# A fused pair of row layers on one core: the third stage issued in program order, ten rows deep, with the right matrix applied to four row sums at once

## The chip, the cores and the metric

The kernel runs on one core of one Trainium2 chip. The metric is the device time in microseconds of one execution. Times of single instructions come from one profiled execution. "PE" is TensorE (matmuls), "PEld" its weight loads, "DVE" VectorE, "ACT" ScalarE, "POOL" GpSimd, "SP" the engine from which the DMA transfers are issued.

## The reference

The input x has the shape 1×384×384×128, in float32: rows i, columns j, 128 channels. Two layers are applied, one after the other.

```python
# layer 0
z = layernorm(x) ; left = (z@Wl+bl)*sigmoid(z@Wlg+blg) ; right = (z@Wr+br)*sigmoid(z@Wrg+brg)
core = einsum('bikh,bjkh->bijh', left, right)
x1 = x + sigmoid(x@Wg+bg) * (layernorm(core)@Wout + bout)
# layer 1, on x1
left = x1@W_left + b_left + x1@W_eq + b_eq
right_sum = sum over j of (x1@W_right + b_right)        # one vector for each row i
out = (left * right_sum * sigmoid(x1@W_gate + b_gate)) @ W_out + b_out
y = layernorm(out + x1) * ln_scale + ln_bias
```

Since the sum over j and the product with W_right can change places, a row needs only its 128 channel sums ("tot") multiplied by W_right ("rsum").

## The kernel before, in words

There are three stages. The first normalises x and writes left and right to DRAM. The second multiplies them channel by channel, writes core to DRAM and gathers what the normalisation of core needs. The third, which the change touches, runs over the 384 rows i. It holds a row transposed, with the channels on the 128 partitions and the 384 columns j along the free dimension, and does the rest of layer 0 and all of layer 1.

A row passes through these steps. The names are those of the tiles, the line numbers those of the profile.

- L361, L363: three PE transposes of x into the PSUM tile pxt, and ACT's copy of it to xT. L364: POOL multiplies core by its reciprocal deviation, cs.
- L303, L305: PE multiplies xT by Wg into pg; ACT takes the sigmoid, gT.
- L324, L325, L328: PE multiplies cs by the output matrix into pr; DVE multiplies by gT, then adds xT, which gives x1T and, as a by-product, its sum over j, tot.
- L309, L315, L317: PE multiplies the one column tot by the right matrix; DVE adds the bias, rsum; ACT scales the output matrix with it, wo.
- L310, L313, L311, L319: PE multiplies x1T by the gate matrix into pg2 (the profile shows it as pg, too) and by the left matrix into pl; ACT takes the sigmoid g2; DVE forms u.
- L341, L342: for each of three blocks of 128 columns, PE multiplies u by wo into py and adds the transposed x1T to it. Py has the columns j on the partitions. L347, L349: DVE's statistics of py.
- L351, L352, L355: for every two rows, POOL forms the reciprocal deviations rs, and DVE nm, which is minus the mean times rs.
- L370, L373, L376: ACT normalises py in three instructions, DVE multiplies by the scale, POOL adds the bias, into yt.

Rows are loaded and stored four at a time from SP. The function tick(t) writes down, for one value of t, the steps of six rows: r0 is row t, r1 row t-1, and so on up to r5. Each step belongs to one of these. The rows overlap in this way, and a step's input was mostly made a tick before. The order in the text is pg of r1, layer 1's products of r2, pr of r1, py of r3, the transposes of r0, and the normalisation of r5.

The order of issue on each engine is not that of the text. The kernel is built with `schedule_with_timeline_sim=True`: a scheduler orders each engine's instructions by a simulated time, within the dependencies. Each tile name of a pool rotates over the pool's number of buffers; all products of the third stage but py share one rotation of four PSUM banks ("bank"), and py has four banks of its own.

Of the kernel before, what the change touches and what calls it, by code (L numbers as in the profile page):

```python
# [8 lines left out]
F32 = mybir.dt.float32  # L9
AF = mybir.ActivationFunctionType  # L10
ALU = mybir.AluOpType
# [3 lines left out]
P = 128  # L15
EPS = 1e-5
# [3 lines left out]
def triangle_then_gated_row_kernel(ctx: ExitStack, tc: tile.TileContext, a: dict, out: bass.AP):  # L20
# [18 lines left out]
    RG = 4  # L39
# [3 lines left out]
    lr_d = dpool.tile([H, N, N, 2], F32, name="lr_d")  # L43
    core_d = dpool.tile([N, H, N], F32, name="core_d")
    rstd_d = dpool.tile([N, N], F32, name="rstd_d")


    def const(shape, name):
# [2 lines left out]
    def load(dst, src):  # L51
        nc.sync.dma_start(out=dst, in_=src)
# [11 lines left out]
    ident = const([P, P], "ident")  # L64
# [25 lines left out]
    wc = const([P, C], "wc")  # L90
    bz = const([P, 1], "bz")
    with tc.tile_pool(name="prep", bufs=1) as pp, tc.tile_pool(name="prep_ps", bufs=1, space=PSUM) as ps:
# [3 lines left out]
        d = pp.tile([P, 1], F32, name="d")  # L96
# [29 lines left out]
    with tc.tile_pool(name="p1x", bufs=3) as xp, tc.tile_pool(name="p1lr", bufs=2) as lrp, \  # L126
# [5 lines left out]
        loaded, normed = {}, {}  # L132
# [135 lines left out]


    with tc.tile_pool(name="p3in", bufs=3) as inp, tc.tile_pool(name="p3out", bufs=3) as op, \  # L270
         tc.tile_pool(name="p3w", bufs=4) as wp, tc.tile_pool(name="p3s", bufs=4) as sp, \
# [6 lines left out]
        def work(name):  # L278
            return wp.tile([P, N], F32, tag=name, name=name)
# [4 lines left out]
        loaded, rows, yts, pair = {}, {}, {}, {}  # L284

        def load_rows(i0):
            if i0 < N:
                xt = inp.tile([P, RG, NB, C], F32, tag="xt", name="xt")
                load(xt, x[i0:i0 + RG].rearrange("i (b p) c -> p i b c", p=P))
                ct = inp.tile([P, RG, N], F32, tag="ct", name="ct")  # L290
                load(ct, core_d[i0:i0 + RG].rearrange("i h j -> h i j"))
                rt = inp.tile([P, RG, N], F32, tag="rt", name="rt")
                load(rt.rearrange("p i j -> p (i j)"),
                     rstd_d[i0:i0 + RG].rearrange("i j -> (i j)").partition_broadcast(P))
                loaded[i0] = xt, ct, rt

        def tick(t):

            r0, r1, r2, r3, r4, r5 = (rows.get(t - d) for d in range(6))
            if r1:  # L300

                pg = bank("pg")
                nc.tensor.matmul(pg[:, :N], lhsT=wg0, rhs=r1["xT"], start=True, stop=True)  # L303
                gT = work("gT")
                nc.scalar.activation(gT, pg[:, :N], AF.Sigmoid, bias=bg0)  # L305
            if r2:

                pl, pg2 = bank("pl"), bank("pg2")
                nc.tensor.matmul(pl[:, N:N + 1], lhsT=wright, rhs=r2["tot"], start=True, stop=True)  # L309
                nc.tensor.matmul(pg2[:, :N], lhsT=wgate, rhs=r2["x1T"], start=True, stop=True)  # L310
                nc.tensor.matmul(pl[:, :N], lhsT=wleft, rhs=r2["x1T"], start=True, stop=True)  # L311
                g2 = work("g2")
                nc.scalar.activation(g2, pg2[:, :N], AF.Sigmoid, bias=bgate)  # L313
                rsum = sp.tile([P, 1], F32, tag="rsum", name="rsum")
                nc.vector.tensor_add(rsum, pl[:, N:N + 1], bright)  # L315
                wo = wp.tile([P, C], F32, tag="wo", name="wo")
                nc.scalar.activation(wo, wout1, AF.Copy, scale=rsum)  # L317
                u = work("u")
                nc.vector.scalar_tensor_tensor(u, pl[:, :N], bleft, g2, ALU.add, ALU.mult)  # L319
                r2.update(u=u, wo=wo)  # L320
            if r1:

                pr = bank("pr")
                nc.tensor.matmul(pr[:, :N], lhsT=wc, rhs=r1["cs"], start=True, stop=True)  # L324
                nc.vector.scalar_tensor_tensor(pr[:, :N], pr[:, :N], bz, gT, ALU.add, ALU.mult)  # L325
                x1T = work("x1T")
                tot = sp.tile([P, 1], F32, tag="tot", name="tot")
                nc.vector.scalar_tensor_tensor(  # L328
                    x1T, pr[:, :N], bout1, r1["xT"], ALU.add, ALU.add, accum_out=tot
                )  # L330
                r1.update(x1T=x1T, tot=tot)
            if r3:

                m, n = divmod(t - 3, 2)
# [4 lines left out]
                py = ps2.tile([P, 512], F32, tag="py", name="py")  # L339
                for s in cols:  # L340
                    nc.tensor.matmul(py[:, s], lhsT=r3["u"][:, s], rhs=r3["wo"], start=True, stop=False)  # L341
                    nc.tensor.matmul(  # L342
                        py[:, s], lhsT=r3["x1T"][:, s], rhs=ident, start=False, stop=True, is_transpose=True
                    )
                st = sp.tile([P, NB, 6], F32, tag="st", name="st")
                for b in range(NB):
                    nc.vector.bn_stats(st[:, b, :], py[:, cols[b]])  # L347
                for b in range(NB):
                    nc.vector.bn_aggr(mv[:, n, b, :], st[:, b, :])  # L349
                if n == 1:  # L350
                    nc.gpsimd.tensor_scalar(rs, mv[:, :, :, 1], EPS, 1.0, ALU.add, ALU.mult)  # L351
                    nc.gpsimd.tensor_tensor(  # L352
                        rs, rs, mhalf[:, :2 * NB].rearrange("p (a b) -> p a b", b=NB), ALU.pow
                    )
                    nc.vector.scalar_tensor_tensor(nm, mv[:, :, :, 0], -1.0, rs, ALU.mult, ALU.mult)  # L355
                r3.update(py=py, rs=rs[:, n], nm=nm[:, n])
            if r0:

                pxt = bank("pxt")
                for b, s in enumerate(cols):  # L360
                    nc.tensor.transpose(pxt[:, s], r0["x"][:, b, :], ident)  # L361
                xT, cs = work("xT"), work("cs")
                nc.scalar.copy(xT, pxt[:, :N])  # L363
                nc.gpsimd.tensor_tensor(cs, r0["c"], r0["r"], ALU.mult)  # L364
                r0.update(xT=xT, cs=cs)
            if r5:

                py, yt = r5["py"], r5["y"]
                for b, s in enumerate(cols):
                    nc.scalar.activation(  # L370
                        py[:, s], py[:, s], AF.Identity, bias=r5["nm"][:, b:b + 1], scale=r5["rs"][:, b:b + 1]
                    )
                nc.vector.tensor_tensor(  # L373
                    yt, py[:, :N].rearrange("p (b c) -> p b c", b=NB), lnsb, ALU.mult
                )
                nc.gpsimd.tensor_tensor(yt, yt, lnbb, ALU.add)  # L376

        load_rows(0)
        load_rows(RG)
        for t in range(N + 5):  # L380
            if t < N:
                r = t % RG
                if r == 0:
                    load_rows(t + 2 * RG)
                    xt, ct, rt = loaded.pop(t)
                    yt = op.tile([P, RG, NB, C], F32, tag="yt", name="yt")
                    yts[t] = yt
                rows[t] = {"x": xt[:, r], "c": ct[:, r], "r": rt[:, r], "y": yt[:, r]}
            tick(t)
            done = t - 5  # L390
            rows.pop(done, None)
            if done >= 0 and done % RG == RG - 1:
                i0 = done - RG + 1
                nc.sync.dma_start(out=y[i0:i0 + RG].rearrange("i (b p) c -> p i b c", p=P), in_=yts.pop(i0))


_INS = [
# [26 lines left out]
```

## Time and profile before

| what | value |
|---|---|
| time, median of 3 runs | 3922.84 us (3920.99 to 3922.89) |
| the profiled execution's own time | 3925.36 us |
| its span, first to last instruction | 3923.6 us |
| mean granted TensorE clock | 0.974 |
| second stage, first to last matmul | 1398 to 2180 us |
| third stage, from its first transpose on | 2208 us to the end |
| busy from 2300 to 2500 us | PE 198.98, DVE 152.56, ACT 138.95, POOL 123.99 us of 200 |
| core busy over the span | PE 93%, DVE 71%, ACT 50%, POOL 32% |

In the profile's slices a digit is the busy share in tenths of one fortieth of the span, some 98 us. A group of instructions is listed as line, engine, operation, output and inputs, shapes and count, then its busy time in us and the mean duration of one in ns, then the idle time of the engine just ahead of it, with what ended that. A line of the timeline has the start in us, the duration, the engine, the line and the number of instructions merged into it; in brackets the idle time before it. Matmuls are pipelined: one starts before the last one's recorded end, so that the distance between starts, not the duration, is what one takes of PE.

### The profile page before, as it was taken

How to read it: one execution, taken by the hardware profiler on the slowest of the kernel's cores; microseconds unless marked ns; L12 is line 12 of the kernel's file. 1: busy time of each engine (PE TensorE's matmuls, PEld its weight loads, DVE VectorE, ACT ScalarE, POOL GpSimd, SP SyncE). 2: the span in 40 equal slices, each digit the busy share in tenths (PEclk: the TensorE clock that was granted, in tenths of full speed). 3: DMA queues.
4: the chain of work that ended last, by engine and by line, in shares of the span. 5: the costliest groups of instructions: out<-in, count | busy, mean ns of one | idle time of the engine just before them, and what ended most of it. 6: DMA issues, size and time to landing. Idle time of an engine off the chain costs nothing.

```text
span 3923.6 us, 46929 instructions
## 1 busy us (share of the span) xinstructions
PE 3668.2 (93%) x14222; PEld 2190.0 (56%) x14222; DVE 2768.9 (71%) x9123; ACT 1952.0 (50%) x3815; POOL 1272.4 (32%) x1304
## 2 busy tenths in 40 slices
PE   7888998998898879999999699999999999999998
PEld 3444443444443345555555466666676676667665
DVE  7878888887887724444444577777777777777776
ACT  2333333333333323333333366666666666666666
POOL 2111111111111100000000266666666666666665
PEclk9999999999999989999999899999999999999999
DMA  3575565565466499999999555555565655556562
GB/s 92 164 200 143 156 199 160 148 199 169 140 194 172 137 287 292 291 293 290 292 290 290 195 170 185 175 180 183 172 192 166 190 173 182 178 177 186 170 192 82
DMA packets 802259, 759.46 MB, mean 194 GB/s; under 512 B 13524, under 2 KB 703704, under 8 KB 802008
## 3 DMA queue, kind: packets, MB, share of 16 engines
q1 hardware_dynamic: 802008, 756.47, 63.6%
q8 instruction: 114, 1.87, 0.2%
q14 instruction: 137, 1.12, 0.1%
HBM read 453.84 MB, written 302.58 MB: 193 GB/s over the span
## 4 chain that ended last, share of the span: by engine, by line
PE 63%; DVE 19%; DMA 16%; ACT 1%; POOL 1%; SPq 0%; issue 0%; POOLq 0%; DVEq 0%; ACTq 0%
PE pc L239 20%; DMA xt<-in_x_dram 15%; PE py L341 8%; PE pg L303 7%; PE pg L310 7%; DVE lr L186 7%; PE pr L324 6%; PE pl L311 6%; DVE st L151 5%; DVE z L165 4%; PE pxt L361 3%; PE py L342 3%; DVE mv L153 2%; PE pr L182 1%; PE pl L309 1%; DMA lr_d<-lr 1%
## 5 line engine op out<-in xcount | busy, mean ns | idle before, releaser
L182 PE MATMUL pr<-wz,zt 128*128 128x512 f32 x2304 | 1098.9, 615 | 137.0 <-DVE lr L186 134.9
L239 PE MATMUL pc<-lrh 128*128 128x384 f32 x2304 | 782.2, 500 | 37.9 <-DMA lrh<-lr_d 37.9
L184 ACT ACTIVATE sg<-pr 128x512 f32<-128x512 f32 x576 | 343.9, 597 | 842.6 <-PE pr L182 755.5
L182 PEld LDWEIGHTS pr<-wz,zt 128*128 128x128 f32 x2304 | 417.4, 195 | 607.5 <-issue 383.2
L364 POOL TENSOR_TENSOR cs<-ct,rt 128x384 f32<-128x384 f32 x384 | 384.3, 1001 | 912.2 <-ACT gT L305 874.3
L239 PEld LDWEIGHTS pc<-lrh 128*128 128x128 f32 x2304 | 448.1, 195 | 372.2 <-issue 41.1
L186 DVE TENSOR_TENSOR lr<-pr,sg 128x512 f32<-128x512 f32 x576 | 588.6, 1027 | 36.4 <-ACT sg L184 36.4
L248 DVE TENSOR_TENSOR csum<-csum,ct 128x1152 f32<-128x1152 f32 x128 | 173.9, 1358 | 486.0 <-ACT ct L245 486.0
L376 POOL TENSOR_TENSOR yt<-yt,lnb 128x384 f32<-128x384 f32 x384 | 374.9, 997 | 393.8 <-DVE yt L373 390.9
L370 ACT ACTIVATE py<-py,nm,rs 128x128 f32<-128x128 f32 x1152 | 435.4, 442 | 53.3 <-DVE nm L355 53.3
L341 PE MATMUL py<-wo,u 128*128 128x128 f32 x2304 | 431.7, 287 | 1.1 <-DVE u L319 0.9
L245 ACT COPY ct<-pc 128x1152 f32<-128x1152 f32 x128 | 143.3, 1119 | 525.2 <-PE pc L239 525.2
L341 PEld LDWEIGHTS py<-wo,u 128*128 128x128 f32 x2304 | 346.2, 190 | 41.4 <-ACT wo L317 2.3
L155 POOL TENSOR_SCALAR rs<-mv 128x16 f32<-128x16 f32 x72 | 14.7, 204 | 1079.3 <-DVE mv L153 1079.3
L165 DVE TENSOR_SCALAR z<-xt,mv,rs 128x128 f32<-128x128 f32 x1152 | 324.2, 338 | 42.9 <-PE pt L168 42.9
L305 ACT ACTIVATE gT<-pg,col_L_conv_bg 128x384 f32<-128x384 f32 x384 | 229.1, 597 | 251.1 <-PE pg L303 251.1
L151 DVE BATCH_NORM_STATS2 st<-xt 128x6 f32<-128x128 f32 x1152 | 253.2, 275 | 138.7 <-DMA xt<-in_x_dram 138.5
L303 PE MATMUL pg<-xT,mat_L_conv_Wg 128*128 128x384 f32 x768 | 332.4, 515 | 12.3 <-ACT xT L363 12.3
L310 PE MATMUL pg<-x1T,mat_L_conv_W_gate 128*128 128x384 f32 x768 | 343.2, 529 | 0.0
L342 PE MATMUL py<-ident,x1T 128*128 128x128 f32 x1152 | 314.0, 273 | 0.0
L324 PE MATMUL pr<-cs,wc 128*128 128x384 f32 x768 | 312.0, 488 | 2.1 <-POOL cs L364 2.1
L311 PE MATMUL pl<-x1T,mat_L_conv_W_left 128*128 128x384 f32 x768 | 311.2, 487 | 0.0
(78 smaller groups left out, 4763.8 us busy)
## 6 DMA issues: line engine op xcount, KB each, us to landing
lr_d<-lr SPq DMA_DIRECT2D x18, 8192.0 KB, 31.1
lrh<-lr_d SPq DMA_DIRECT2D x128, 1152.0 KB, 9.1
core_d<-ct SPq DMA_DIRECT2D x128, 576.0 KB, 3.8
xt<-in_x_dram SPq DMA_DIRECT2D x96, 768.0 KB, 8.2
ct<-core_d SPq DMA_DIRECT2D x96, 768.0 KB, 8.8
rt<-rstd_d SPq DMA_DIRECT2D x96, 768.0 KB, 7.2
out_dram<-yt SPq DMA_DIRECT2D x96, 768.0 KB, 7.4
xt<-in_x_dram SPq DMA_DIRECT2D x72, 0.5 KB, 6.6
```

What stands on the lines that cost most here:

```text
L151: nc.vector.bn_stats(st[:, r, :], loaded[n][:, r, :])
L165: nc.vector.tensor_scalar(z[:, r, :], xt[:, rr, :], mv[:, rr, 0:1], rs[:, rr:rr + 1], ALU.subtract, ALU.mult)
L182: nc.tensor.matmul(pr[:, r, :], lhsT=zt[:, 2 * h2 + r, :], rhs=wz, start=True, stop=True)
L186: nc.vector.tensor_tensor(t[:, :, i0:i0 + 2, :].rearrange("k h i s -> k i s h"), pr[:, :, :2 * H].rearrange("k i (s h) -> k i s h", s=2), ...
L239: nc.tensor.matmul(pc[:, ib, :N], lhsT=t[:, kb, ib * P:(ib + 1) * P, 0], rhs=t[:, kb, :, 1], start=(kb == 0), stop=(kb == NB - 1),)
L303: nc.tensor.matmul(pg[:, :N], lhsT=wg0, rhs=r1["xT"], start=True, stop=True)
L310: nc.tensor.matmul(pg2[:, :N], lhsT=wgate, rhs=r2["x1T"], start=True, stop=True)
L311: nc.tensor.matmul(pl[:, :N], lhsT=wleft, rhs=r2["x1T"], start=True, stop=True)
L324: nc.tensor.matmul(pr[:, :N], lhsT=wc, rhs=r1["cs"], start=True, stop=True)
L341: nc.tensor.matmul(py[:, s], lhsT=r3["u"][:, s], rhs=r3["wo"], start=True, stop=False)
L342: nc.tensor.matmul(py[:, s], lhsT=r3["x1T"][:, s], rhs=ident, start=False, stop=True, is_transpose=True)
L370: nc.scalar.activation(py[:, s], py[:, s], AF.Identity, bias=r5["nm"][:, b:b + 1], scale=r5["rs"][:, b:b + 1])
```

## The change

Every instruction of the third stage is passed through `tc.keep_in_program_order`, which puts it behind the instruction that the program text has before it on the same engine: the scheduler no longer reorders this stage. The DMA issues on SP are included. No instruction is added by this.

A row is spread over ten ticks in place of five. In tick t, PE's text order is now: pg of row t-1; in every fourth tick the right product pq of four rows; pr of row t-2; pg2 and pl of row t-3; py of row t-7; the transposes of row t. ACT's is: gT (t-1), wo (t-6), g2 (t-3), three normalisations (t-9), the copy xT (t). DVE's is: the scaling (t-10), rsum in every fourth tick, the two products of pr (t-2), nm in every second tick (t-9), u (t-3), the statistics (t-7). POOL's is: the bias (t-10), cs (t), and rs in every second tick (t-7). The row sums of four rows are gathered in one 128×4 tile "tot", multiplied by the right matrix in one matmul with four columns, and rsum is made for four rows in one DVE instruction. x1T and u get seven buffers, as they now live longer. The output tile yt is taken when its first row is finished rather than when the row is loaded.

```diff
+    def seq(ins):
+        return tc.keep_in_program_order(ins)
...
+         tc.tile_pool(name="p3w", bufs=4) as wp, tc.tile_pool(name="p3l", bufs=7) as lp, \
...
-                load(xt, x[i0:i0 + RG].rearrange("i (b p) c -> p i b c", p=P))
+                seq(nc.sync.dma_start(out=xt, in_=x[i0:i0 + RG].rearrange("i (b p) c -> p i b c", p=P)))
...
+        D = 10
...
+            r = [rows.get(t - d) for d in range(D + 1)]
+            if r[1]:
+                pg = bank("pg")
+                seq(nc.tensor.matmul(pg[:, :N], lhsT=wg0, rhs=r[1]["xT"], start=True, stop=True))
+                gT = r[1]["gT"] = work("gT")
+                seq(nc.scalar.activation(gT, pg[:, :N], AF.Sigmoid, bias=bg0))
+            if r[D]:
...
+                seq(nc.vector.tensor_tensor(
+                    yt, r[D]["py"][:, :N].rearrange("p (b c) -> p b c", b=NB), lnsb, ALU.mult
+                ))
+                seq(nc.gpsimd.tensor_tensor(yt, yt, lnbb, ALU.add))
+            if t >= 6 and (t - 6) % 4 == 0 and (t - 6) // 4 in quad:
+                q = quad[(t - 6) // 4]
+                pq = bank("pq")
+                seq(nc.tensor.matmul(pq[:, :4], lhsT=wright, rhs=q["tot"], start=True, stop=True))
+                q["rsum"] = sp.tile([P, 4], F32, tag="rsum", name="rsum")
+                seq(nc.vector.tensor_scalar(q["rsum"], pq[:, :4], bright, None, ALU.add))
+            if r[2]:
...
+                seq(nc.tensor.matmul(pr[:, :N], lhsT=wc, rhs=r[2]["cs"], start=True, stop=True))
+                seq(nc.vector.scalar_tensor_tensor(pr[:, :N], pr[:, :N], bz, r[2]["gT"], ALU.add, ALU.mult))
+                x1T = r[2]["x1T"] = work("x1T", lp)
+                seq(nc.vector.scalar_tensor_tensor(
+                    x1T, pr[:, :N], bout1, r[2]["xT"], ALU.add, ALU.add, accum_out=quad[m]["tot"][:, n:n + 1]
+                ))
+            if r[9]:
...
+                    seq(nc.vector.scalar_tensor_tensor(nm, mv[:, :, :, 0], -1.0, rs, ALU.mult, ALU.mult))
+            if r[6]:
...
+                seq(nc.scalar.activation(wo, wout1, AF.Copy, scale=quad[m]["rsum"][:, n:n + 1]))
+            if r[3]:
...
-                nc.tensor.matmul(pl[:, N:N + 1], lhsT=wright, rhs=r2["tot"], start=True, stop=True)
...
+                seq(nc.tensor.matmul(pg2[:, :N], lhsT=wgate, rhs=r[3]["x1T"], start=True, stop=True))
+                seq(nc.tensor.matmul(pl[:, :N], lhsT=wleft, rhs=r[3]["x1T"], start=True, stop=True))
...
+            if r[0]:
+                cs = r[0]["cs"] = work("cs")
+                seq(nc.gpsimd.tensor_tensor(cs, r[0]["c"], r[0]["r"], ALU.mult))
+            if r[7]:
...
                 for s in cols:
+                    seq(nc.tensor.matmul(py[:, s], lhsT=r[7]["u"][:, s], rhs=r[7]["wo"], start=True, stop=False))
+                    seq(nc.tensor.matmul(
+                        py[:, s], lhsT=r[7]["x1T"][:, s], rhs=ident, start=False, stop=True, is_transpose=True
+                    ))
...
+            if r[9]:
...
+                for b, s in enumerate(cols):
+                    seq(nc.scalar.activation(
+                        py[:, s], py[:, s], AF.Identity, bias=nm[:, n, b:b + 1], scale=rs[:, n, b:b + 1]
+                    ))
+            if r[0]:
                 pxt = bank("pxt")
                 for b, s in enumerate(cols):
-                    nc.tensor.transpose(pxt[:, s], r0["x"][:, b, :], ident)
...
+                    seq(nc.tensor.transpose(pxt[:, s], r[0]["x"][:, b, :], ident))
+                xT = r[0]["xT"] = work("xT")
+                seq(nc.scalar.copy(xT, pxt[:, :N]))
...
-        for t in range(N + 5):
+        for t in range(N + D):
```

More of the change, by code (lines that the diff above doesn't have):

```diff
@@ L270, in triangle_then_gated_row_kernel @@
     with tc.tile_pool(name="p3in", bufs=3) as inp, tc.tile_pool(name="p3out", bufs=3) as op, \
-         tc.tile_pool(name="p3w", bufs=4) as wp, tc.tile_pool(name="p3s", bufs=4) as sp, \
+         tc.tile_pool(name="p3w", bufs=4) as wp, tc.tile_pool(name="p3l", bufs=7) as lp, \
+         tc.tile_pool(name="p3s", bufs=4) as sp, \
          tc.tile_pool(name="p3ps", bufs=4, space=PSUM) as ps, \
@@ L276, in bank, with work @@
             return ps.tile([P, 512], F32, tag="bank", name=name)
-        def work(name):
-            return wp.tile([P, N], F32, tag=name, name=name)
+        def work(name, pool=wp):
+            return pool.tile([P, N], F32, tag=name, name=name)
         cols = [slice(b * P, (b + 1) * P) for b in range(NB)]
@@ L283, in triangle_then_gated_row_kernel @@
         lnbb = lnb.unsqueeze(1).to_broadcast([P, NB, C])
-        loaded, rows, yts, pair = {}, {}, {}, {}
+        loaded, rows, yts, pair, quad = {}, {}, {}, {}, {}
         def load_rows(i0):
@@ L288, in load_rows @@
                 xt = inp.tile([P, RG, NB, C], F32, tag="xt", name="xt")
-                load(xt, x[i0:i0 + RG].rearrange("i (b p) c -> p i b c", p=P))
+                seq(nc.sync.dma_start(out=xt, in_=x[i0:i0 + RG].rearrange("i (b p) c -> p i b c", p=P)))
                 ct = inp.tile([P, RG, N], F32, tag="ct", name="ct")
-                load(ct, core_d[i0:i0 + RG].rearrange("i h j -> h i j"))
+                seq(nc.sync.dma_start(out=ct, in_=core_d[i0:i0 + RG].rearrange("i h j -> h i j")))
@@ L292, in load_rows @@
                 rt = inp.tile([P, RG, N], F32, tag="rt", name="rt")
-                load(rt.rearrange("p i j -> p (i j)"),
-                     rstd_d[i0:i0 + RG].rearrange("i j -> (i j)").partition_broadcast(P))
+                seq(nc.sync.dma_start(
+                    out=rt.rearrange("p i j -> p (i j)"),
+                    in_=rstd_d[i0:i0 + RG].rearrange("i j -> (i j)").partition_broadcast(P),
+                ))
                 loaded[i0] = xt, ct, rt
+        D = 10
         def tick(t):
-            r0, r1, r2, r3, r4, r5 = (rows.get(t - d) for d in range(6))
@@ L300, in tick @@
-            if r1:
+            r = [rows.get(t - d) for d in range(D + 1)]
+            if r[1]:
                 pg = bank("pg")
[L303 to L311, printed above, removed]
-                g2 = work("g2")
[L313 to L331, printed above, removed]
@@ L332, in tick @@
-            if r3:
-                m, n = divmod(t - 3, 2)
+                seq(nc.tensor.matmul(pg[:, :N], lhsT=wg0, rhs=r[1]["xT"], start=True, stop=True))
+                gT = r[1]["gT"] = work("gT")
+                seq(nc.scalar.activation(gT, pg[:, :N], AF.Sigmoid, bias=bg0))
+            if r[D]:
+                if (t - D) % RG == 0:
+                    yts[t - D] = op.tile([P, RG, NB, C], F32, tag="yt", name="yt")
+                yt = yts[(t - D) // RG * RG][:, (t - D) % RG]
+                seq(nc.vector.tensor_tensor(
+                    yt, r[D]["py"][:, :N].rearrange("p (b c) -> p b c", b=NB), lnsb, ALU.mult
+                ))
+                seq(nc.gpsimd.tensor_tensor(yt, yt, lnbb, ALU.add))
@@ new lines, in tick @@
+            if t >= 6 and (t - 6) % 4 == 0 and (t - 6) // 4 in quad:
[5 more added lines that the diff above has]
+            if r[2]:
+                m, n = divmod(t - 2, 4)
+                if n == 0:
+                    quad[m] = {"tot": sp.tile([P, 4], F32, tag="tot", name="tot")}
+                pr = bank("pr")
+                seq(nc.tensor.matmul(pr[:, :N], lhsT=wc, rhs=r[2]["cs"], start=True, stop=True))
[4 more added lines that the diff above has]
+                ))
@@ new lines, in tick @@
+            if r[9]:
+                m, n = divmod(t - 9, 2)
+                mv, rs, nm = pair[m]
+                if n == 0:
+                    seq(nc.vector.scalar_tensor_tensor(nm, mv[:, :, :, 0], -1.0, rs, ALU.mult, ALU.mult))
+            if r[6]:
+                wo = r[6]["wo"] = wp.tile([P, C], F32, tag="wo", name="wo")
+                m, n = divmod(t - 6, 4)
+                seq(nc.scalar.activation(wo, wout1, AF.Copy, scale=quad[m]["rsum"][:, n:n + 1]))
+            if r[3]:
+                pg2, pl = bank("pg2"), bank("pl")
+                seq(nc.tensor.matmul(pg2[:, :N], lhsT=wgate, rhs=r[3]["x1T"], start=True, stop=True))
+                seq(nc.tensor.matmul(pl[:, :N], lhsT=wleft, rhs=r[3]["x1T"], start=True, stop=True))
+                g2 = work("g2")
+                seq(nc.scalar.activation(g2, pg2[:, :N], AF.Sigmoid, bias=bgate))
+                u = r[3]["u"] = work("u", lp)
+                seq(nc.vector.scalar_tensor_tensor(u, pl[:, :N], bleft, g2, ALU.add, ALU.mult))
@@ L335, in tick @@
+            if r[0]:
+                cs = r[0]["cs"] = work("cs")
+                seq(nc.gpsimd.tensor_tensor(cs, r[0]["c"], r[0]["r"], ALU.mult))
+            if r[7]:
+                m, n = divmod(t - 7, 2)
                 if n == 0:
@@ L338, in tick @@
                 mv, rs, nm = pair[m]
-                py = ps2.tile([P, 512], F32, tag="py", name="py")
+                py = r[7]["py"] = ps2.tile([P, 512], F32, tag="py", name="py")
                 for s in cols:
[L341 to L344, printed above, removed]
+                    seq(nc.tensor.matmul(py[:, s], lhsT=r[7]["u"][:, s], rhs=r[7]["wo"], start=True, stop=False))
+                    seq(nc.tensor.matmul(
+                        py[:, s], lhsT=r[7]["x1T"][:, s], rhs=ident, start=False, stop=True, is_transpose=True
+                    ))
@@ L345, in tick @@
                 st = sp.tile([P, NB, 6], F32, tag="st", name="st")
                 for b in range(NB):
-                    nc.vector.bn_stats(st[:, b, :], py[:, cols[b]])
+                    seq(nc.vector.bn_stats(st[:, b, :], py[:, cols[b]]))
                 for b in range(NB):
-                    nc.vector.bn_aggr(mv[:, n, b, :], st[:, b, :])
+                    seq(nc.vector.bn_aggr(mv[:, n, b, :], st[:, b, :]))
                 if n == 1:
-                    nc.gpsimd.tensor_scalar(rs, mv[:, :, :, 1], EPS, 1.0, ALU.add, ALU.mult)
@@ L352, in tick @@
-                    nc.gpsimd.tensor_tensor(
+                    seq(nc.gpsimd.tensor_scalar(rs, mv[:, :, :, 1], EPS, 1.0, ALU.add, ALU.mult))
+                    seq(nc.gpsimd.tensor_tensor(
                         rs, rs, mhalf[:, :2 * NB].rearrange("p (a b) -> p a b", b=NB), ALU.pow
[L354 to L357, printed above, removed]
+                    ))
@@ L359, in tick @@
+            if r[9]:
+                m, n = divmod(t - 9, 2)
+                mv, rs, nm = pair[m]
+                py = r[9]["py"]
+                for b, s in enumerate(cols):
+                    seq(nc.scalar.activation(
+                        py[:, s], py[:, s], AF.Identity, bias=nm[:, n, b:b + 1], scale=rs[:, n, b:b + 1]
+                    ))
+            if r[0]:
                 pxt = bank("pxt")
                 for b, s in enumerate(cols):
-                    nc.tensor.transpose(pxt[:, s], r0["x"][:, b, :], ident)
@@ L362, in tick @@
[L362 to L376, printed above, removed]
+                    seq(nc.tensor.transpose(pxt[:, s], r[0]["x"][:, b, :], ident))
@@ L385, in triangle_then_gated_row_kernel @@
                     xt, ct, rt = loaded.pop(t)
-                    yt = op.tile([P, RG, NB, C], F32, tag="yt", name="yt")
-                    yts[t] = yt
-                rows[t] = {"x": xt[:, r], "c": ct[:, r], "r": rt[:, r], "y": yt[:, r]}
+                rows[t] = {"x": xt[:, r], "c": ct[:, r], "r": rt[:, r]}
             tick(t)
-            done = t - 5
+            done = t - D
             rows.pop(done, None)
@@ L393, in triangle_then_gated_row_kernel @@
                 i0 = done - RG + 1
-                nc.sync.dma_start(out=y[i0:i0 + RG].rearrange("i (b p) c -> p i b c", p=P), in_=yts.pop(i0))
+                seq(nc.sync.dma_start(out=y[i0:i0 + RG].rearrange("i (b p) c -> p i b c", p=P), in_=yts.pop(i0)))
 _INS = [
```

## The prediction

> **What bounds the kernel now.** I read the page first: the slices, then the chain.
>
> ```profile
> PE   7888998998898879999999699999999999999998
> PEclk9999999999999989999999899999999999999999
> ...
> PE 63%; DVE 19%; DMA 16%; ACT 1%; POOL 1%; SPq 0%; issue 0%; POOLq 0%; DVEq 0%; ACTq 0%
> ```
>
> The third stage begins at slice 23 and has PE busy in every tenth at the full clock (the windows view grants 1.00 from 2300 us on). The end is set by PE, so the change is worth what it does to PE's own sequence. Next, the groups of the stretch 2240 to 3900 us, kept apart by shape:
>
> ```profile
> L370 ACT ACTIVATE py<-py,nm,rs 128x128 f32<-128x128 f32 x1134 | 428.8, 442 | 48.5 <-DVE nm L355 48.5
> ...
> L303 PE MATMUL pg<-xT,mat_L_conv_Wg 128*128 128x384 f32 x754 | 325.0, 513 | 11.2 <-ACT xT L363 11.2
> ...
> L363 ACT COPY xT<-pxt 128x384 f32<-128x384 f32 x377 | 182.1, 483 | 70.9 <-PE pxt L361 70.9
> ...
> L309 PE MATMUL pl<-tot,mat_L_conv_W_right 128*128 128x1 f32 x754 | 104.9, 209 | 0.0
> ```
>
> A product of float32 operands is two passes (754 for 377 rows), a transpose one. PE's idle time is almost nothing (11.2 us), so the row time must be read from distances between starts. The waits of the same stretch name the only producer that PE meets:
>
> ```profile
> ACT xT L363 <- PE pxt L361: 70.9, 188, 0.4
> ...
> PEld pg L303 <- ACT xT L363: 50.2, 189, 1.3
> ACT py L370 <- DVE nm L355: 48.5, 189, 1.3
> ```
>
> Every second row, the weight load of pg waits for ACT's copy xT of the transposed x. The timeline shows an odd row without that wait, then an even one with it:
>
> ```profile
> 3002.15 0.49 PE L361 MATMUL pxt<-ident,xt 128*128 128x128 f32 x3
> ...
> 3002.68 0.48 ACT L363 COPY xT<-pxt 128x384 f32<-128x384 f32 x1 [0.38 <-PE pxt L361]
> ...
> 3003.61 0.81 PE L303 MATMUL pg<-xT,mat_L_conv_Wg 128*128 128x384 f32 x2
> ...
> 3006.41 0.49 PE L361 MATMUL pxt<-ident,xt 128*128 128x128 f32 x3
> ...
> 3006.76 0.78 ACT L370 ACTIVATE py<-py,nm,rs 128x128 f32<-128x128 f32 x2 [0.19 <-DVE nm L355]
> 3006.80 0.46 PE L341 MATMUL py<-wo,u 128*128 128x128 f32 x2
> ...
> 3007.46 0.48 ACT L363 COPY xT<-pxt 128x384 f32<-128x384 f32 x1
> ...
> 3007.99 0.30 PEld L303 LDWEIGHTS pg<-xT,mat_L_conv_Wg 128*128 128x128 f32 x2 [0.21 <-ACT xT L363]
> 3008.00 0.91 PE L303 MATMUL pg<-xT,mat_L_conv_Wg 128*128 128x384 f32 x2
> 3008.74 0.28 PE L309 MATMUL pl<-tot,mat_L_conv_W_right 128*128 128x1 f32 x2
> 3008.89 0.89 PE L310 MATMUL pg<-x1T,mat_L_conv_W_gate 128*128 128x384 f32 x2
> 3009.61 0.81 PE L311 MATMUL pl<-x1T,mat_L_conv_W_left 128*128 128x384 f32 x2
> ```
>
> The decisive reading is the order on PE. In the program text the transposes (L361) come behind py and end the tick; in the trace they were issued ahead of py (3002.15 against 3002.53). So 1.1 us of py work lies between pxt and the pg that needs its copy, and the copy is hidden, but for the even rows.
>
> **The row now, from starts** (ns, medians over the rows of 2300 to 3890 us). From the third transpose to py 167; first py pass to last py transpose 961; from there to pg 109 (odd) or 239 (even); pg's first pass 325 or 427, its second 322; right 28+112; pg2 406+322; pl 323+322; pr 323+322; the first two transposes 218. Mean of both rows: 4376. The period of pg's starts agrees: 4362 and 4392 in turn, plus a hitch of 1.05 us in 11 rows.
>
> **The right matrix four rows at a time.** One-column right costs 28+112 itself, and 406-322 = 84 on pg2, whose weight load (190 ns, its group's mean) has no long pass to hide behind: 224 ns per row. Four in one leave 224/4 = 56, a gain of 168. Four columns are not in the trace: the bounds per pass are 28 (one column) and 109 (128 columns), at most 2×81/4 = 40 more per row; I take 28, the nearest row. For the one-column product the Trainium skill (TensorE: Matmul & The Clock Gate, the part on back-to-back issue) gives an issue floor of about 25 ns per matmul, which agrees with the 28 ns between the passes but would put the gain at an estimated 0.75×50 = 38 ns a row, 14 us in all; the trace's 224, with the weight loads in it, decides. The sum on DVE (158 ns, L315) falls to one in four; DVE is busy 76% in the stage, so this is worth nothing.
>
> **The pinned order.** Every instruction now stays behind the previous one of its engine. PE's tick becomes pg, (pq), pr, pg2, pl, py, pxt: the transposes go back to the end, with pg of the same row as PE's next work. Nothing covers the copy any more. From the third transpose's start: 309 to ACT's copy (3002.68 less 3002.37), 478 for the copy, 53 to pg (measured in every even row), so 840 before pg, against 109 with data at hand: a hole of 731 per row. Pg's first pass then takes 427, not 325, in every row, as its weight load waits as well: 102. Together 833, where now a mean of (130+102)/2 = 116 is lost: a loss of 717. Behind pg everything on PE waits in its order, so nothing fills the hole.
>
> The transposes' other neighbours: 167 to py goes, 109 from py to pxt comes: a gain of 58. The first pair of py passes is 186 apart now, the others 112; behind pl's long pass it may be 112 too, so 0 to 74 gained; I take 0, as its weight load cannot start before the first pass does.
>
> **Is ACT ready for the copy?** The three normalisations now stand ahead of it in every tick. Counted from pg's start: pg's second pass 427, gT at 427+523 = 950 (523 from last pass to ACT, L305 and L313 alike), over at 1530; wo to about 1930; pg2's second pass at 749+645+322 = 1716, g2 at 2239; normalisations from about 2800 at 343 each, free by 3830. In ticks with nm: DVE's first product at pr's second pass 1071+523 = 1594, x1T 657 later, its accumulator read 542 later, nm at about 2877, ACT 190 behind it, free at about 4100. The copy is due at 749+645+645+645+961+109+218+309 = 4281. ACT is early by 180 at least, which covers it; without that cover every 100 ns late costs 38 us over 384 rows.
>
> **What else moves, at no cost.** u, wo, x1T, cs and tot are now made a tick or more ahead of PE's use; their waits were not PE's in the trace. Five or six PSUM banks a tick over four buffers: each taker follows its old reader by over half a tick. DVE's work (about 3.5 us a row), POOL's (1.0+1.0, and 1.5 every second row) and ACT's (3.4) fit a longer tick. SP's loads and stores keep their places, two groups (8 rows, over 35 us) ahead of a landing of 7 to 9 us; they hide behind that. Ten drain ticks in place of five: the rows' PE work is counted above, and the ticks with py alone run at POOL's pace, (997+1533/2) against 1070: about 0.7 us for 7 ticks, 5 us; bounds 0 and 10. The hitch on nm (1.05 us, 11 times) may now be partly absorbed: 0 to 11 us less; I take 0.
>
> **Sum.** Per row -168 -58 +717 = +491 ns; 384 rows give 188.5 us, plus 5: +193.5. The profiled execution's 3925.36 us (span 3923.6) would become 4118.9; from the median, 3922.84, 4116. Added the other way, the new row is 749+645×3+961+109+218+840+56 = 4868 ns.
>
> PE then idles some 0.73 us per row. In this trace the clock fell to 0.5 after PE's last work before the third stage (from 4.6 us behind it, for 37.5 us) and in stretches of 7 to 10 us in the first stage, but stays full in the third. The Trainium skill (TensorE: Matmul & The Clock Gate, the table on what matters for kernels) warns of gaps over about 3 us; no gap of that length arises by my count, and no run here shows where the limit is.
>
> **Rivals.** (1) Faster: the transposes still reach PE ahead of pg by 731 ns or more, as the present trace has them, so that the pin does not do what it says. Then only the right part counts: -168×384 = -64.5 us, 3858; with the even rows' 116 gone as well, 3814. For it: the present trace shows exactly this order. Against: pg and pxt are both PE instructions, and each is tied to the one before. Below 731 ns of cover the copy shows; the sign turns where the hole is about 240 (168+58+116-102).
> (2) Slower still: ACT comes late, since g2, nm and three normalisations now precede the copy in each row. For it: the even rows' copy stood behind two normalisations at 3006.76. Against: the 180 ns above. If the chain were 430 longer in every second row, 250 late: +48 us, 4164.
> (3) The clock falls in the holes: a tenth of the stage's 4.0 us of PE work per row at half speed is 0.4×384 = 154 us, 4270. Against: the first stage's slices of 7 and 8 tenths stand at clock 9.
>
> **How the numbers follow.** My forecast has 0.82, rival 1 0.05, rival 2 0.09, rival 3 0.02; 0.02 is for what I don't see. The low end takes the 74 of py (28 us), the hitch (11) and no drain cost (5): 4072. The high end takes four columns at full price (15 us) and about 30 us of rival 2: 4160. This leaves out about 1 in 10. About 0.2% is what a measurement of this kernel tells from no change. Faster 0.05 (rival 1), same 0.01, slower 0.94.
>
> **What would show it.** Right: PE's order pg, pr, pg2, pl, py, pxt; an idle stretch before pg in every row, ended by ACT xT, with the copy 309 behind the third transpose; starts of pg 4.8 to 4.9 us apart; one pq in four rows; PE busy falling to about 8 tenths at clock 9; DVE, ACT and POOL waiting more. Wrong: pxt ahead of py; the copy starting behind a normalisation rather than behind PE; half-clock stretches; holes before any other PE line.

## The result, and the profile after

The changed kernel took 4243.0 us (median of 4 runs, 4242.36 to 4243.59) against 3921.91 before: a ratio of 1.0819, 95% interval 1.08 to 1.0838. It is 321 us slower, where 194 were forecast with 4160 us as the end of the range. The direction and the place were right; the size was not.

The page of the kernel after, slices and chain:

```profile
PE   7989888998987899999978888887888888888886
PEclk9999999999999999999989999999999999999999
...
PE 45%; DVE 31%; DMA 14%; ACT 8%; issue 1%; SPq 0%; POOL 0%; POOLq 0%; DVEq 0%; ACTq 0%
```

PE has fallen from a full 9 to 8 tenths in the third stage, at the same clock. The chain that ended last has moved in part from PE (63% before) to DVE (19% before, now 31%) and ACT (1% to 8%). The waits of the stretch 2300 to 4200 us:

```profile
PEld pg L312 <- ACT xT L402: 453.9, 363, 1.7
...
ACT py L393 <- DVE nm L347: 179.6, 181, 1.0
```

Now every one of the 363 rows waits for the copy (the forecast's step). But in every second row the normalisations also wait, up to 1.0 us, for nm, which the forecast had ready. The groups show why: nm is one instruction on 128x6 elements, and its mean is 971 ns, where it was 202 before. First the line of the kernel before (2240 to 3900 us):

```profile
L355 DVE SCALAR_TENSOR_TENSOR nm<-mv,rs 128x6 f32<-128x6 f32 x188 | 38.0, 202 | 1.8 <-POOL rs L352 1.8
```

Then the kernel after (2240 to 4220 us):

```profile
L393 ACT ACTIVATE py<-py,nm,rs 128x128 f32<-128x128 f32 x1134 | 486.6, 429 | 212.5 <-DVE nm L347 187.2
L312 PE MATMUL pg<-xT,mat_L_conv_Wg 128*128 128x384 f32 x752 | 343.2, 538 | 380.4 <-ACT xT L402 273.5 <-DVE mv L382 106.9
...
L347 DVE SCALAR_TENSOR_TENSOR nm<-mv,rs 128x6 f32<-128x6 f32 x190 | 184.5, 971 | 1.5 <-POOL rs L385 1.5
```

A row without nm, then one with it, in the timeline (engines' lines picked out in order of time):

```profile
3003.95 0.49 PE L400 MATMUL pxt<-ident,xt 128*128 128x128 f32 x3
...
3004.47 0.48 ACT L402 COPY xT<-pxt 128x384 f32<-128x384 f32 x1
...
3005.01 0.91 PE L312 MATMUL pg<-xT,mat_L_conv_Wg 128*128 128x384 f32 x2 [0.57 <-DVE mv L382]
...
3007.76 1.00 POOL L364 TENSOR_TENSOR cs<-ct,rt 128x384 f32<-128x384 f32 x1
...
3007.81 0.98 DVE L347 SCALAR_TENSOR_TENSOR nm<-mv,rs 128x6 f32<-128x6 f32 x1
...
3008.69 0.49 PE L400 MATMUL pxt<-ident,xt 128*128 128x128 f32 x3
...
3008.82 1.36 ACT L393 ACTIVATE py<-py,nm,rs 128x128 f32<-128x128 f32 x3 [0.99 <-DVE nm L347]
...
3010.10 0.48 ACT L402 COPY xT<-pxt 128x384 f32<-128x384 f32 x1
```

In the first row the third transpose starts at 3003.95 + 0.22 = 3004.17, the copy 0.3 behind it, pg 0.84 behind it: as forecast. (The bracket of pg names DVE's mv, which ran at that time; pg reads xT, and the waits above put its weight load down to the copy in all 363 rows.) In the second the copy starts not behind PE but behind the third normalisation, 1.19 after the third transpose. The normalisations waited for nm, and nm began while POOL was in cs and ended 21 ns after it (3007.806 + 0.979 against 3007.760 + 1.004).

In starts (ns, from the trace): the period of pg is 4738 in rows with neither pq nor nm, 4962 with pq, and 5632 with nm; rows with nm are half of all.

### The profile page after: what moved, and what is told of

The parts are those of the page before. It is cut to its first block, busy times and chain, and to the rows that moved or that the text cites. A ratio compares the mean times of both kernels' runs of the same rounds, so it can differ in the third digit from the quotient of the medians.

```text
span 4241.0 us, 45695 instructions
## 1 busy us (share of the span) xinstructions
PE 3607.9 (85%) x13646; PEld 2138.1 (50%) x13646; DVE 2898.8 (68%) x8835; ACT 1985.7 (47%) x3815; POOL 1265.4 (30%) x1304
## 4 chain that ended last, share of the span: by engine, by line
PE 45%; DVE 31%; DMA 14%; ACT 8%; issue 1%; SPq 0%; POOL 0%; POOLq 0%; DVEq 0%; ACTq 0%
PE pc L243 18%; DMA xt<-in_x_dram 13%; PE pg L312 8%; DVE lr L190 7%; PE pr L337 6%; ACT py L393 6%; DVE st L155 5%; DVE nm L347 4%; DVE z L169 4%; DVE st L380 3%; PE py L374 3%; PE pg L356 3%; PE pl L357 3%; DVE pr L338 3%; DVE x1T L340 3%; ACT xT L402 2%
## 5 line engine op out<-in xcount | busy, mean ns | idle before, releaser
L312 PE MATMUL pg<-xT,mat_L_conv_Wg 128*128 128x384 f32 x768 | 352.7, 541 | 385.2 <-ACT xT L402 277.7
L393 ACT ACTIVATE py<-py,nm,rs 128x128 f32<-128x128 f32 x1152 | 494.2, 429 | 221.2 <-DVE nm L347 195.5
L338 DVE SCALAR_TENSOR_TENSOR pr<-pr,bz,gT 128x384 f32<-128x384 f32 x384 | 240.3, 626 | 420.6 <-PE pr L337 420.6
L374 PEld LDWEIGHTS py<-wo,u 128*128 128x128 f32 x2304 | 379.1, 191 | 106.0 <-ACT py L393 2.8
L374 PE MATMUL py<-wo,u 128*128 128x128 f32 x2304 | 405.0, 276 | 4.5 <-ACT py L393 2.4
L312 PEld LDWEIGHTS pg<-xT,mat_L_conv_Wg 128*128 128x128 f32 x768 | 114.8, 188 | 476.7 <-ACT xT L402 476.7
```

Of the source, the lines that this page charges most:

```text
L312: seq(nc.tensor.matmul(pg[:, :N], lhsT=wg0, rhs=r[1]["xT"], start=True, stop=True))
L338: seq(nc.vector.scalar_tensor_tensor(pr[:, :N], pr[:, :N], bz, r[2]["gT"], ALU.add, ALU.mult))
L374: seq(nc.tensor.matmul(py[:, s], lhsT=r[7]["u"][:, s], rhs=r[7]["wo"], start=True, stop=False))
L393: seq(nc.scalar.activation(py[:, s], py[:, s], AF.Identity, bias=nm[:, n, b:b + 1], scale=rs[:, n, b:b + 1]))
```

## The experiments

Each run is compared with runs of the kernel before on the same chip; these were 3926 to 3928 us.

**1. nm off DVE.** Nm is made by two POOL instructions behind rs.

```diff
-                    seq(nc.vector.scalar_tensor_tensor(nm, mv[:, :, :, 0], -1.0, rs, ALU.mult, ALU.mult))
...
+                    seq(nc.gpsimd.tensor_scalar(nm, mv[:, :, :, 0], 0.0, -1.0, ALU.add, ALU.mult))
+                    seq(nc.gpsimd.tensor_tensor(nm, nm, rs, ALU.mult))
```

> The changed kernel, with nm made by two small POOL instructions directly behind rs, not by DVE behind the accumulator read of x1T. Theory (the extra loss sits in every second row, whose normalisations wait for a 980 ns nm on DVE): the copy xT is due 309 ns behind the last transpose again, ACT being free about 100 ns earlier; every row then takes 4738 ns, or 4962 with pq, and the 894 ns of the nm rows go: 4243 - 0.894*192 = 4071 us. Rival (the spacing of 463 ns of the three normalisations is enough to make the copy late by itself): about half of it stays, 4150 us or more.

Measured: 4078.66 us, ratio 1.0388 (1.0373 to 1.0404). The rows take 4738 or 4962 ns, none more, and the copy starts 138 ns of ACT idle time behind the last normalisation. Put on the same base, (1.0819 - 1.0388) × 3922 = 169 us go, for a forecast 172. So the loss beyond the uncovered copy hangs on nm; with nm ready this early, the 463 ns between the normalisations do not make the copy late (experiment 4 shows what they cost otherwise).

**2. The same place, one SBUF tensor per instruction.**

```diff
-                    seq(nc.vector.scalar_tensor_tensor(nm, mv[:, :, :, 0], -1.0, rs, ALU.mult, ALU.mult))
+                    for k in range(2):
+                        for b in range(NB):
+                            seq(nc.vector.tensor_scalar(
+                                nm[:, k, b:b + 1], mv[:, k, b, 0:1], rs[:, k, b:b + 1], -1.0, ALU.mult, ALU.mult
+                            ))
```

> The changed kernel, with nm made at the same place on DVE, but as six one-column instructions, each with one tensor from SBUF and two scalars, in place of one instruction that reads two tensors (mv and rs) from SBUF. Theory (an instruction with two SBUF tensors is held until POOL's running instruction is over): the six start at once, 80 to 150 ns apart, the normalisations start 250 to 450 ns earlier, the nm rows lose about 0.25 to 0.45 us: 4160 to 4195 us. Rival (what stands behind the accumulator read is late, whatever it is): the first of the six takes some 980 ns, time 4243 us or more.

Measured: 4101.71 us, ratio 1.0446 (1.0431 to 1.0462). That is better than I expected, as the first normalisation needs only the first of the six. The timeline of this kernel:

```profile
3006.17 1.00 POOL L368 TENSOR_TENSOR cs<-ct,rt 128x384 f32<-128x384 f32 x1
...
3006.22 0.81 DVE L349 TENSOR_SCALAR nm<-mv,rs 128x1 f32<-128x1 f32 x6
...
3006.47 1.36 ACT L397 ACTIVATE py<-py,nm,rs 128x128 f32<-128x128 f32 x3 [0.23 <-DVE nm L349]
```

They start behind the same accumulator read and beside the same cs, and run at once, some 205 ns each. What stands ahead of nm is thus not the cause; its second SBUF tensor or POOL is.

**3. POOL idle as nm comes up (the condition did not come about).** The bias addition to yt on POOL was left out.

```diff
-                seq(nc.gpsimd.tensor_tensor(yt, yt, lnbb, ALU.add))
```

> The changed kernel without POOL's bias addition to yt (left out, so that POOL is idle when nm comes up; nm itself stays the same instruction at the same place on DVE). Theory (nm is held until POOL's running instruction is over): POOL's cs now ends at about 2800 ns of the tick, as nm comes up; nm takes 160 to 250 ns, ACT is free about 70 to 170 ns after the copy is due, in place of 893: 4085 to 4105 us. Rival (nm is slow where it follows the accumulator read): nm stays at 980 ns, 4243 us.

Measured: 4239.82 us, ratio 1.0796 (1.078 to 1.0813). The time speaks for the rival, but the trace shows that POOL was not idle: with less to do it ran ahead, and the cs of the next row fell on nm. The timeline of this kernel:

```profile
2999.71 1.96 POOL L363 TENSOR_TENSOR cs<-ct,rt 128x384 f32<-128x384 f32 x2
...
3000.73 0.96 DVE L346 SCALAR_TENSOR_TENSOR nm<-mv,rs 128x6 f32<-128x6 f32 x1
```

Nm ends 20 ns behind the second cs, and 186 of the 192 nm begin inside a cs. The edit had not made the condition that it was to test.

**4. POOL idle, mended.** The same nm at the same place; only POOL's cs is moved, two rows at a time into the ticks without nm.

```diff
-            if r[0]:
-                cs = r[0]["cs"] = work("cs")
-                seq(nc.gpsimd.tensor_tensor(cs, r[0]["c"], r[0]["r"], ALU.mult))
+            if r[0] and t % 2 == 0:
+                for row in (r[0], rows[t + 1]):
+                    cs = row["cs"] = work("cs")
+                    seq(nc.gpsimd.tensor_tensor(cs, row["c"], row["r"], ALU.mult))
```

> The changed kernel with nothing moved but POOL's cs: the cs of rows t and t+1 are both made in the ticks with rs, ahead of it, so that in the ticks with nm POOL has only the end of rs and the bias addition, which is over at about 2800 ns, as nm comes up. The nm instruction and its place on DVE are unchanged. Theory (nm is held by the POOL instruction that runs when it comes up): nm takes 160 to 200 ns, the normalisations start at about 2990, at 463 ns from one to the next, ACT is free at 4275, 68 behind the due 4207, in place of 893: 4243 - 0.825*192 = 4085 us. Rival (nm is slow behind the accumulator read whatever POOL does): nm 980 ns, 4243 us.

Measured: 4095.32 us, ratio 1.0429 (1.0412 to 1.0447). The timeline of this kernel:

```profile
3003.15 0.99 POOL L323 TENSOR_TENSOR yt<-yt,lnb 128x384 f32<-128x384 f32 x1
...
3004.15 0.16 DVE L347 SCALAR_TENSOR_TENSOR nm<-mv,rs 128x6 f32<-128x6 f32 x1
...
3004.34 1.36 ACT L394 ACTIVATE py<-py,nm,rs 128x128 f32<-128x128 f32 x3 [0.17 <-DVE nm L347]
...
3005.63 0.48 ACT L403 COPY xT<-pxt 128x384 f32<-128x384 f32 x1
```

POOL ends at 3004.14, nm starts behind it and takes 0.16. The rows with nm take 4814 ns in place of 5632: the 76 above 4738 are the normalisations, which by their 463 ns end that much after the copy is due (68 expected). This settles the theory: nm comes up at 2800 ns of the tick in both kernels, and the same instruction takes 160 or 980 ns by what POOL does. All nm of the two traces agree: after, 191 of 192 are long and end 19 to 26 ns behind a POOL instruction; here 188 of 192 begin at or behind the end of POOL's instruction (at most 3 ns ahead of it) and take 159 to 164. The other four begin inside POOL's bias addition, take 951 to 955 and end 21 to 23 ns behind it.

The Trainium skill (SBUF — State Buffer, the sections on SBUF's two separate sides and on who interferes with whom) says that a DVE instruction with two SBUF inputs reads the second through an interface shared with GpSimd, and that against a GpSimd instruction that reads SBUF whichever starts first holds it for its whole instruction. For a DVE instruction that starts second the runs above agree, with 0.82 us as the price; nm is the one DVE instruction of this tick with two SBUF tensors, as the others read PSUM or one tensor. That POOL is held in its turn no run here shows: the 178 cs of the kernel before that began inside a short nm took 1001 ns in the median, as the others did.

**5. The normalisations' spacing.** Tried in the faster order of experiment 6 with nm on POOL: the blocks of two rows are normalised in turn.

```diff
-                for b, s in enumerate(cols):
-                    seq(nc.scalar.activation(
-                        py[:, s], py[:, s], AF.Identity, bias=nm[:, n, b:b + 1], scale=rs[:, n, b:b + 1]
-                    ))
+                if n == 0:
+                    for b, s in enumerate(cols):
+                        for k, py in enumerate((r[9]["py"], r[8]["py"])):
+                            seq(nc.scalar.activation(
+                                py[:, s], py[:, s], AF.Identity, bias=nm[:, k, b:b + 1], scale=rs[:, k, b:b + 1]
+                            ))
```

> The kernel with the transposes ahead of py and nm on POOL, with the normalisations of a pair of rows made in one tick, block by block in turn from the one row and the other, so that no two in succession write the same PSUM tile. Theory (an instruction in place on a PSUM tile waits for the end of the one before it on that tile): starts 343 to 350 ns apart instead of 463, and no idle 33 ns between them; the time about the same, 3767 us, or a little more where six in one tick make gT late. Rival (the spacing comes from the bias and scale operands): 463 again.

Measured, one run: 3777.8 us. In its timeline six normalisations take 2.19 us:

```profile
3005.03 2.19 ACT L398 ACTIVATE py<-py,nm,rs 128x128 f32<-128x128 f32 x6
```

That is (2.19 - 0.46)/5 = 0.35 from start to start, against (1.36 - 0.43)/2 = 0.46 for the three of one row above. In place on the same PSUM tile, each starts 33 ns behind the end of the last; from two tiles in turn they overlap. The second and third of a row carry a wait on ACT's own semaphore in the trace, and so do those of two tiles in turn; which count they wait for is not recorded. The 33 ns may thus be a wait that the program sets rather than the engine's own; this was not tried. The forecast's 343 came from the kernel before, where the six of two rows run together with 340 to 360 ns from start to start; that the scheduler had mixed the two rows there is inferred from this, as the trace does not tell their tiles apart.

**6. The transposes ahead of py, still pinned.** The block with pxt and the copy xT is moved up, whole, between the block of r[3] and the cs of r[0].

> The changed kernel, still pinned, with the transposes and the copy xT written between pl and py, not behind py and the normalisations. Theory (the loss is the uncovered copy, with what stands ahead of it on ACT): PE has 1.1 us of py between the last transpose and pg, the copy stands ahead of the normalisations; the row falls to 4037 + 56 = 4093 ns, which is 3818 us with 5 us of drain, if DVE and ACT keep up; late nm and normalisations then delay nobody on PE. Rival (ten rows' spread with pins makes DVE or ACT the bound): above 3920 us.

Measured: 3767.81 us, ratio 0.9594 (0.958 to 0.9608): faster than both kernels, and 50 us below my expectation. The waits of 2300 to 3700 us no longer hold one of pg. The windows view of 3000 to 3200 us (the stretch, its length, then busy us and instructions of PE, PEld, DVE, ACT and POOL, clock, DMA share, GB/s):

```profile
3000.00:3200.00 200.00, 200.00 (x1037) 144.16 (x1036) 180.90 (x595) 155.80 (x355) 137.04 (x152) 1.00 0.62 202
```

PE is busy for 200 of 200 us. The period is 3907 ns, 4131 with pq, on average 3963; it is below 4093 since py behind the transposes starts at 109, not 167 (58 less), and its first two passes are 112 apart like the others (74 less). Nm still takes 0.96 us here, and nobody on PE waits for it.

**7. The same with nm on POOL.**

> The kernel with the transposes and the copy ahead of py, and nm made by POOL besides. Theory (there the normalisations are off PE's path, so a late nm costs nothing): the same time as without the second edit, 3768 us, within 6. Rival (nm still delays what PE needs): 3750 us or less.

Measured: 3766.92 us, ratio 0.9593 (0.9577 to 0.9609). The period is the same as in 6. The long nm costs only where it stands ahead of what PE waits for.

**8. The same with one row sum at a time.** The product, one column wide, and rsum are made in every tick.

```diff
-            if t >= 6 and (t - 6) % 4 == 0 and (t - 6) // 4 in quad:
...
-                seq(nc.tensor.matmul(pq[:, :4], lhsT=wright, rhs=q["tot"], start=True, stop=True))
...
+            if r[6]:
...
+                seq(nc.tensor.matmul(pq[:, :1], lhsT=wright, rhs=quad[m]["tot"][:, n:n + 1], start=True, stop=True))
```

> The same kernel (transposes and copy ahead of py, nm on POOL), with the right matrix applied to one row sum in every tick instead of to four in every fourth. Theory (one small product costs PE 28 + 112 ns, and 84 on the first pass behind it): 0.75 * 224 = 168 ns more per row, 64.5 us: 3832 us. Rival (the weight loads are hidden, and only the passes count, 28 ns each): 0.75 * 56 * 0.384 = 16 us more.

Measured: 3829.74 us, ratio 0.9753 (0.9738 to 0.9768); (0.9753 - 0.9593) × 3926 = 63 us more than 7. Every row now takes 4131 ns, in place of 3907 three times in four: 224 per product, as the forecast had it.

**9. The pins alone, on the kernel before.** Every instruction of its third stage goes through the pin; nothing else is changed.

```diff
+    class Pinned:
...
+            return lambda *a, **k: tc.keep_in_program_order(getattr(self.engine, op)(*a, **k))
```

> The kernel before with nothing but the pins: every instruction of its third stage in the order of its text (five ticks, one right product per row; the copy xT stands ahead of the normalisations on ACT). Theory (the uncovered copy costs 840 ns from the last transpose to pg, and 427 in place of 325 on pg's first pass, whatever the number of ticks): row 749 + 140 + 728 + 645 + 645 + 887 + 109 + 218 + 840 = 4961 ns against 4377, 4150 us. Rival (the pins alone are harmless, the loss needs the ten-row order): under 3950 us.

Measured: 4308.5 us, ratio 1.097 (1.0954 to 1.0987). Every second row takes 4962 ns, one above the expectation; the others 5855, as PE waits there for POOL as well. PE's lines of the timeline:

```profile
3002.20 0.91 PE L275 MATMUL pg<-xT,mat_L_conv_Wg 128*128 128x384 f32 x2 [0.57 <-ACT xT L275]
...
3005.25 0.91 PE L275 MATMUL pr<-cs,wc 128*128 128x384 f32 x2 [0.62 <-POOL cs L275]
```

(All lines are L275 here, that of the helper.) In the text before, cs stands behind rs on POOL; pinned, it comes too late for pr in ticks with rs. So pins on that text cost 381 us, and the ten-row text, with 321, takes back 60 of it, about what its four sums at once are worth in experiment 8 (63).

**10. The ten-row text without the pins.**

> The changed kernel without the pins: the text of ten rows and the four sums at once, but the scheduler orders each engine. Theory (the pins bring the loss, by fixing the transposes behind py): the transposes are issued ahead of py again, time 3815 to 3860 us. Rival (the spread over ten rows brings it): above 4000 us.

Measured: 4126.96 us, ratio 1.0509 (1.0491 to 1.0526). My theory fell. The scheduler puts the transposes ahead of py in one row of four only: rsum now comes for four rows at once, and the py of four rows are issued in a bunch. In the other three rows nothing lies between the transposes and pg. From the waits of 2300 to 4050 us:

```profile
PEld pg L312 <- ACT xT L402: 340.0, 267, 1.7
```

267 of 355 rows wait for the copy; the periods are 3743, 4235, 6118 and 5660 ns in turn (medians). The same uncovered copy is reached by another way: what costs is the order on PE, not the pin as such.

## Why the prediction was right or wrong

- **The right matrix**: right. 224 ns per product on PE, in experiment 8 to the nanosecond; a pass with four columns takes the 28 of one column (28 in the trace after).
- **The uncovered copy**: right. From the third transpose to pg 840 to 842 in rows without nm, pg's first pass 427 in every row. Moving the transposes takes it away (experiment 6).
- **py behind pl**: the bound that I did not take. The first pair is 109 to 110 apart, so 74 ns per row are gained, 28.4 us. The reason for taking 0 did not bear: the second pass's weight load does start with the first pass (1 to 2 ns behind it, 190 long), but the second pass starts at 109 all the same.
- **Is ACT ready for the copy?** This is the step that failed. "ACT is early by 180 at least" rested on two sizes read from the order before. Nm was taken as short as it mostly is before (155 ns, with ACT 190 behind its start); it was 980 since the new order brings it up while POOL is in cs. The normalisations were taken at 343 ns; back to back on one row they are 463 apart. Against the forecast the first normalisation starts 748 ns late (3815 against 3067 in the tick), and the three take 252 more (1285 against 1033). Of these 1000 ns the true slack covers 107 (181 by the forecast, and the copy is due 74 sooner, as py is shorter); 893 ns are left, in half the rows: 171 us. The prediction's own sign of being wrong, a copy that starts behind a normalisation, is thus there in every second row. With a short nm the spacing alone costs 76 ns (experiment 4); without the spacing nm alone would cost some 640 by this count, which was not run.

In the kernel before, nm mostly starts first, and POOL's cs behind it:

```profile
3006.57 0.15 DVE L355 SCALAR_TENSOR_TENSOR nm<-mv,rs 128x6 f32<-128x6 f32 x1
...
3006.66 1.00 POOL L364 TENSOR_TENSOR cs<-ct,rt 128x384 f32<-128x384 f32 x1 [0.16 <-PE pr L324]
```

In 11 of the 192 it does not, and the whole chain that the forecast missed can be read there, one row at a time:

```profile
3103.06 1.00 POOL L364 TENSOR_TENSOR cs<-ct,rt 128x384 f32<-128x384 f32 x1
...
3103.12 0.96 DVE L355 SCALAR_TENSOR_TENSOR nm<-mv,rs 128x6 f32<-128x6 f32 x1 [0.16 <-POOL rs L352]
...
3104.12 0.78 ACT L370 ACTIVATE py<-py,nm,rs 128x128 f32<-128x128 f32 x2 [1.25 <-DVE nm L355]
...
3104.82 0.49 ACT L363 COPY xT<-pxt 128x384 f32<-128x384 f32 x1
...
3105.36 0.59 PE L303 MATMUL pg<-xT,mat_L_conv_Wg 128*128 128x384 f32 x1 [1.02 <-ACT xT L363]
```

- **The sum.** 193.5 + 171.5 - 28.4 = 336.6, measured 321.1. Of the 15.5 left, 11.5 are the hitch, which is gone: the profile before has 11 long nm (0.96 us), one for each hitch, and all of them end 19 to 23 ns behind a cs of POOL. The trace before had thus shown the price of a nm that meets POOL, and I carried it along as "the hitch on nm" without asking what ended it. Of the last 4 us, some 3 are the two ends of the stage, which cost about 2 us net in the traces where 5 were forecast; the rest is within the scatter of the kernel before (3920.51 to 3925.36 us).
- **The rivals.** Rival 1 did not happen; its order, made by hand, gives 3768 us. Rival 2 is what happened, at 893 ns where I gave it 250 and 9 in 100; it named nm and the normalisations ahead of the copy, but not what would make nm long. Rival 3 did not: the granted clock is 1.00 from 2218 to 4218 us.

## What to carry to other kernels

Before an order is pinned, write the chain for each producer that PE meets: last input on PE, copy on ACT with all that stands ahead of it there, next user on PE. Durations read in one order do not all hold in another. Those of short DVE instructions with two SBUF tensors depend on what POOL is doing, and those of in-place ACT instructions on who ran just before; a rare long instance of a group in the trace is the price list for this, and its end should be compared with the end of what ran beside it.

The change's two ideas, rows far apart and four sums at once, were sound: with one block moved so that py covers the copy, the same text takes 4.06% less time than the kernel before (ratio 0.9594, 0.958 to 0.9608) and has PE busy for 1400 of the 1400 us from 2300 to 3700.

## What the runs showed of the hardware that I had not expected

- A DVE instruction on six elements per partition took 0.95 to 0.98 us (the medians of the runs) beside a POOL instruction that started before it, and ended some 20 ns after that; when nm started first (before, 178 of 192), it took about 155 ns.
- In-place ACT instructions on one PSUM tile started 463 ns apart, 33 of them idle; on two tiles in turn 343 (median of experiment 5).
- With POOL's bias addition left out, POOL did not stand idle there: it ran ahead and put the next row's cs on the same spot, so that 186 of 192 nm met it (experiment 3).
